# Four layers of cross-attention on one core: tokens laid out by slots of 128, the last group's tokens sent slot by slot, merged values kept in weight buffers

## The chip, the core and the metric

The kernel runs on one core of a Trainium2 chip, everything in fp32 but one small step. A core has a matrix engine (PE, with its weight loads shown apart as PEld), a vector engine (DVE), a scalar engine (ACT), a general one (POOL), and SyncE (SP), which here only issues transfers. Each engine runs its own instructions strictly in order; semaphores hold an instruction until what it needs is there. 16 DMA engines move data between the device memory and the on-chip memory. The latter has 128 partitions, and nearly every tile here spans all of them. The metric is the device time of one execution in microseconds (us). "Before" was measured in three runs; the profile is of one more execution.

## What is computed

2048 tokens of 256 numbers pass through four layers. Each adds a cross-attention over 77 context rows to the tokens, and then a feed-forward. The four differ; the change lies mostly in the last. Cut to it, the reference is:

```python
# layer 3, attention (x: 2 x 1024 x 256, ctx: 2 x 77 x 256, 16 heads)
Q = rope(layernorm(x) @ Wq)                  # 16 heads of 64
K = rope(ctx @ Wk); V = ctx @ Wv             # 4 heads, each used by 4 query heads
scores = Q K^T / 8 + rel_pos_bias[:, abs(i - k)]
scores = where(mask, scores, -1e9)
x = x + concat_heads(softmax(scores) @ V) @ Wo
# layer 3, feed-forward: each token to one of 8 experts, at most 320 tokens each
xf = layernorm(x)
eid = argmax(softmax(xf @ router_w + router_b))
rank = number of earlier tokens with the same eid
valid = rank < 320
y_tok = expert[eid](xf)                      # relu(xf w1 + b1) w2 + b2
yov = relu(xf @ ow1 + ob1) @ ow2 + ob2       # for the tokens that don't fit
out = x + where(valid, y_tok, yov)
```

## The kernel before

**Tokens.** They are cut into 4 groups (`g`) of 512, and a group into 4 slots (`j`) of 128: `xs[g][:, j, :]` is a slot, one token on each partition. Before the change partition `p` and slot `j` hold token 512 g + 4 p + j, so a partition holds four consecutive tokens.

**Order.** The instructions are written as functions per group, slot or head, and a scheduler then reorders them on each engine by a model of their times, within the data's and the buffers' constraints. So the order on an engine is fixed when the kernel is built, but is not that of the source. Transfers of SP stand in one order too: one that waits for a buffer holds all that come after it.

**Weight rooms.** A pool of 6 buffers of 8 KB a partition holds the big weights in turn (`weight(...)`): those of layer 2's feed-forward (gate2T, up2T, down2T), of layer 3's attention (`wkv3`, `wo3`, `wq3`), and then, a megabyte each, the overflow's `ow1`, `ow2` and two for each expert. A load goes out when the tile that had the room has been read for the last time.

**Layer 3's preparation** (`layer3_setup`) runs piece by piece among the pieces of layer 2's feed-forward. It makes the keys (`kblk`), the mask bias (`mb3`) and, for each of the two batches, the product V Wo by head, 1232 rows of 256, which goes to the device memory (`vd`).

**Layer 3's attention** (`layer3_attention`) then begins with loads on SP: the cosines and sines of the queries (`cs`), and `vd` back as `vw` (L913, L916), two tiles of 10 KB a partition in its own pool. After that it is a pipeline over 16 slots (`pipelined`, L1045). In one step, seven stages work on seven successive slots: `ahead` (normalizes and transposes the next group); `queries` (loads the bias tile `rb`, 128 x 16 x 77, L936; adds the mask to it on POOL, L940; query product `pq` on PE, L946; rope on DVE and POOL); `queries_turned` (transposes, L965); `scores` (product, L981; scaling and bias on DVE, L988; softmax by halves of 8 heads, L995 to L1003, whose last step is a multiply on POOL); `last` (`values`: transposes of the weights, L1016, and product with `vw`, L1023, sum into `xs`, L1026); `slot_then` (router logits, for the last group slot by slot, L1117 to L1134, else by group); `after(send)`.

**Sending** (`send`, L1143). For a group: which expert is largest (`largest`), the rank of each token in its expert, whether it overflows, the row that it goes to, and four scatters (L1191), one for each slot, of 513 numbers a token (x, its norm, its index) into the buffer `buf` in the device memory. A rank within the group has two parts: a matmul with a triangular matrix counts the tokens on lower partitions (and one with ones adds `carry`, the count of the groups before); `before` adds up on POOL what the same partition holds in lower slots. The overflow goes the same way with `over` and `os`.

**Experts.** `experts()` reads rows back from `buf` (L1220), for the overflow first (`xe_o`), transposes them (L1229), and runs hidden and answer products for the overflow and the 8 experts. The first read waits for all scatters.

Of the kernel before, what the change touches and what calls it, by code (L numbers as in the profile page):

```python
# [22 lines left out]
F32 = mybir.dt.float32  # L23
# [3 lines left out]
U32 = mybir.dt.uint32  # L27
# [6 lines left out]
P = 128  # L34
D = 256
# [31 lines left out]
def tile_layers(ctx: ExitStack, tc: tile.TileContext, a: dict, out: bass.AP):  # L67
# [26 lines left out]
    def pside(name):  # L94
        return psr.tile([P, 512], F32, tag="pr", name=name)
# [125 lines left out]
    def largest(v, n, name):  # L221

        hot = st.tile([P, J, n], F32, tag="hot", name=f"hot_{name}")
        mx = st.tile([P, J], F32, tag="lmx", name=f"lmx_{name}")
        left = cst[:, C_LEFT : C_LEFT + n].unsqueeze(1).to_broadcast([P, J, n])
        nc.vector.tensor_reduce(mx, v, AX.X, ALU.max)
        nc.vector.tensor_tensor(hot, v, bc(mx, n), ALU.is_equal)
        nc.vector.tensor_tensor(hot, hot, left, ALU.mult)
        nc.vector.tensor_reduce(mx, hot, AX.X, ALU.max)
        nc.vector.tensor_tensor(hot, hot, bc(mx, n), ALU.is_equal)  # L230
        return hot
# [16 lines left out]
    def pipelined(n, *stages):  # L248

        for step in range(n + len(stages) - 1):  # L250
            for k, stage in enumerate(stages):
                if 0 <= step - k < n:
                    stage(step - k)
# [557 lines left out]
    def layer3_setup():  # L811
# [67 lines left out]
        for b, vT in enumerate(vTs):  # L879
# [17 lines left out]
            vds.append(vd)  # L897
        yield wq, mb3, kblk, vds

    def layer3_attention(route, wq, mb3, kblk, vds):  # L900
        with tc.tile_pool(name="a3", bufs=2) as ap, tc.tile_pool(name="a3c", bufs=1) as c3:
            cs = c3.tile([P, 2, 2, J, HD3], F32, name="cs")
            for i in range(2):
# [4 lines left out]
                )  # L908
            vws = []
            for b, vd in enumerate(vds):  # L910
                vw = c3.tile([P, NC3, D], F32, name=f"vw3{b}")
                full = (NC3 - 1) * P
                nc.sync.dma_start(  # L913
                    vw[:, : NC3 - 1, :], vd[:full, :].rearrange("(m p) n -> p m n", p=P)
                )
                nc.sync.dma_start(vw[: H * L - full, NC3 - 1, :], vd[full:, :])  # L916
                vws.append(vw)
            rel = a["relbias"]
# [13 lines left out]
            def queries(it):  # L932
                g, j = divmod(it, J)
                n, gb = f"a3{g}{j}", g % 2
                rb = ap.tile([P, H, L], F32, tag="rb", name=f"rb_{n}")
                nc.sync.dma_start(  # L936
                    rb,
                    bass.AP(rel.tensor, rel.offset + gb * GT + j, [[J, P], [RELW, H], [1, L]]),
                )
# [66 lines left out]
            def values(it):  # L1006
# [15 lines left out]
                for m, w in chunks:  # L1022
                    nc.tensor.matmul(  # L1023
                        po, t[:w, m, :], vws[g // 2][:w, m, :], start=(m == 0), stop=(m == NC3 - 1)
                    )
                nc.vector.tensor_tensor(xs[g][:, j, :], xs[g][:, j, :], po, ALU.add)  # L1026

            def after(f):

                return lambda it: f(it // J) if it % J == J - 1 else None  # L1030

# [12 lines left out]

            pipelined(G * J, ahead, queries, queries_turned, scores, last, slot_then, after(send))  # L1045

# [24 lines left out]
    def layer3_ffn():  # L1071
# [63 lines left out]

        def before(dst, src):

            nc.gpsimd.memset(dst[:, 0], 0.0)
            nc.gpsimd.tensor_copy(dst[:, 1], src[:, 0])
            for j in range(2, J):  # L1140
                nc.gpsimd.tensor_tensor(dst[:, j], dst[:, j - 1], src[:, j - 1], ALU.add)

        def send(g):  # L1143
            n, lg = f"f3{g}", made.pop(g)
            hot = largest(lg, E, n)


            tot = st.tile([P, E], F32, tag="tot3", name=f"tot_{n}")
            nc.vector.tensor_reduce(tot, hot.rearrange("p j e -> p e j"), AX.X, ALU.add)
            pr = pside(f"pr_{n}")[:, :E]  # L1150
            nc.tensor.matmul(pr, tri, tot, start=True, stop=False)
            nc.tensor.matmul(pr, ones, carry, start=False, stop=True)
            nc.vector.tensor_tensor(carry, carry, tot, ALU.add)
            rank = st.tile([P, J, E], F32, tag="rank3", name=f"rank3_{n}")
            before(rank, hot)
            first = st.tile([P, J], F32, tag="first3", name=f"first_{n}")
            sel = st.tile([P, J, E], F32, tag="sel3", name=f"sel_{n}")
            nc.vector.tensor_tensor(
                sel, hot, e320.unsqueeze(1).to_broadcast([P, J, E]), ALU.mult
            )  # L1160
            nc.vector.tensor_reduce(first, sel, AX.X, ALU.add)
            nc.vector.tensor_tensor(
                rank, rank, pr.unsqueeze(1).to_broadcast([P, J, E]), ALU.add
            )
            nc.vector.tensor_tensor(rank, rank, hot, ALU.mult)
            r = st.tile([P, J], F32, tag="r3", name=f"r_{n}")
            nc.vector.tensor_reduce(r, rank, AX.X, ALU.add)

            o = st.tile([P, J, 1], F32, tag="o3", name=f"o_{n}")
            nc.vector.tensor_scalar(o[:, :, 0], r, float(CAP), None, ALU.is_ge)  # L1170
            ot = st.tile([P, 1], F32, tag="ot3", name=f"ot_{n}")
            nc.vector.tensor_reduce(ot, o[:, :, 0], AX.X, ALU.add)
            po = pside(f"pov_{n}")[:, :1]
            nc.tensor.matmul(po, tri, ot, start=True, stop=False)
            nc.tensor.matmul(po, ones, over, start=False, stop=True)
            nc.vector.tensor_tensor(over, over, ot, ALU.add)
            os = st.tile([P, J, 1], F32, tag="os3", name=f"os_{n}")
            before(os, o)

            nc.vector.tensor_tensor(r, r, first, ALU.add)  # L1180
            nc.vector.tensor_tensor(os[:, :, 0], os[:, :, 0], r, ALU.subtract)
            nc.vector.scalar_tensor_tensor(
                os[:, :, 0], os[:, :, 0], po, o[:, :, 0], ALU.add, ALU.mult
            )
            nc.vector.scalar_tensor_tensor(
                r, o[:, :, 0], float(NSLOT), r, ALU.mult, ALU.add
            )
            to = st.tile([P, J], U32, tag="to3", name=f"to_{n}")
            nc.vector.tensor_tensor(to, os[:, :, 0], r, ALU.add)
            for j in range(J):  # L1190
                nc.gpsimd.indirect_dma_start(  # L1191
                    out=next(views),
                    out_offset=bass.IndirectOffsetOnAxis(ap=to[:, j : j + 1], axis=0),
                    in_=tokens[g][:, j, :], in_offset=None,
                )
# [180 lines left out]
    with tc.tile_pool(name="masks", bufs=1) as mp:  # L1376
# [13 lines left out]
        with (  # L1390
# [23 lines left out]
            layer1_attention(weights, beside)  # L1414
            with tc.tile_pool(name="a3s", bufs=2) as sp, tc.tile_pool(name="f2", bufs=2) as fp:
                route, hidden, down = layer2_ffn(fp, gate_up)
                setup.send(sp)


                route(0)  # L1420
                for g in range(G):
                    pieces = [lambda e=e: hidden(g, e) for e in range(E)]
                    pieces += [lambda j=j: down(g, j) for j in range(J)]
                    for k, piece in enumerate(pieces):
                        if g + 2 < G and k < len(chain):
                            chain[k](g + 2)
                        piece()
                        if g < 2 and k % 2 == 1 and k > 4 or (g, k) in ((0, 1), (0, 3)):
                            next(setup)
                        if g + 1 < G and k == E:  # L1430
                            route(g + 1)
                made3 = next(setup)
    route, experts = layer3_ffn()
    layer3_attention(route, *made3)
    experts()

def _constants(np):
# [9 lines left out]
    c[:, C_E320 : C_E320 + E] = CAP * np.arange(E)  # L1449
    token = GT * np.arange(G)[None, :, None] + J * p[:, None, None] + np.arange(J)[None, None, :]  # L1450
    c[:, C_TOKEN : C_TOKEN + G * J] = token.reshape(P, G * J)
# [11 lines left out]


def _laid_out(np, given):
    i = {k: np.asarray(v) for k, v in given.items()}
    o = {k: v for k, v in i.items() if k[0] == "L"}
    o["x"] = i["x"].reshape(NT, D)
    ctx = i["ctx_1024"][:, ::-1]
    o["ctxn"] = ctx  # L1470
    o["ctxT"] = ctx.transpose(2, 0, 1)
    o["mask0"] = i["mask_Bx1xSxS2_bk1"][..., ::-1].reshape(NT, L)
    o["mask1"] = i["mask_Bx1xSxS2_ik1"][..., ::-1].reshape(NT, L)
    o["mask2"] = i["mask_BxSxS2_ik1"][..., ::-1].reshape(NT, L)
    o["mask3"] = i["mask_BxS2_bf1"][:, ::-1]
# [10 lines left out]
    rope = _rope(np)  # L1486
    o["ropeq"] = rope
    o["ropek"] = rope[:, L - 1 :: -1]
# [20 lines left out]
```

## Time and profile before

| | |
|---|---|
| three runs | 1139.82, 1141.12, 1142.36 us (median 1141.12) |
| the profiled execution | 1144.02 us, its span 1141.9 us |
| mean clock granted to PE | 0.957 of full speed |
| PE busy | 1030.9 us, 90% of the span |
| DVE, POOL, ACT busy | 719.7, 384.3, 362.3 us |
| device memory | 55.35 MB read, 19.64 MB written, 66 GB/s |
| from 640 to 701 us (layer 2's feed-forward, end) | PE busy 59.42 of 61.00 us |
| from 701 to 735 us (start of layer 3's attention) | PE busy 28.48 of 34.00 us |
| from 735 to 905 us (most of it) | PE busy 161.12 of 170.00, DVE 133.81, POOL 111.33 |
| from 925 to 946 us (hand-over to the experts) | PE busy 4.88 of 21.00 us, clock 0.62 |
| from 946 us to the end (experts) | PE busy 182.52 of 196.00 us |

The span is that of the instructions; the execution's own time includes what lies around them. In a row of the timeline the first number is the start in us from the beginning of the span, the second its length, then engine, line of the source, operation, output <- inputs, shapes, and "xN" where N alike in a row are put together. The brackets give the idle time of the engine before it and what ended it. "issue" means that the engine waited for nothing that the profile shows. In the row of clocks, and of busy shares, a digit is tenths, and 9 is 90% or more.

### The profile page before, as it was taken

How to read it: one execution, taken by the hardware profiler on the slowest of the kernel's cores; microseconds unless marked ns; L12 is line 12 of the kernel's file. 1: busy time of each engine (PE TensorE's matmuls, PEld its weight loads, DVE VectorE, ACT ScalarE, POOL GpSimd, SP SyncE). 2: the span in 40 equal slices, each digit the busy share in tenths (PEclk: the TensorE clock that was granted, in tenths of full speed). 3: DMA queues.
4: the chain of work that ended last, by engine and by line, in shares of the span. 5: the costliest groups of instructions: out<-in, count | busy, mean ns of one | idle time of the engine just before them, and what ended most of it. 6: DMA issues, size and time to landing. Idle time of an engine off the chain costs nothing.

```text
span 1141.9 us, 13923 instructions
## 1 busy us (share of the span) xinstructions
PE 1030.9 (90%) x4776; PEld 645.4 (57%) x4776; DVE 719.7 (63%) x1849; ACT 362.3 (32%) x1116; POOL 384.3 (34%) x367
## 2 busy tenths in 40 slices
PE   5899989999998887796998999799899958999996
PEld 3355544455444454465664646577678845767774
DVE  6678965776668799949596537668878731222211
ACT  1666620000376563131321110555354511111100
POOL 5633310013333453413120001766566641211211
PEclk9899989999998998897999999999999977999998
DMA  8400038432200000011001005522132223253530
GB/s 266 64 1 1 2 82 143 79 52 45 77 1 1 1 1 28 12 60 48 12 23 60 0 3 184 131 46 56 34 93 62 80 88 93 78 176 100 191 131 18
DMA packets 100279, 74.89 MB, mean 66 GB/s; under 512 B 57916, under 2 KB 90476, under 8 KB 100206
## 3 DMA queue, kind: packets, MB, share of 16 engines
q1 hardware_dynamic: 92974, 58.20, 18.3%
q10 hardware_dynamic: 4800, 9.46, 4.7%
q0 software_dynamic: 2432, 6.31, 1.5%
q8 instruction: 40, 0.66, 0.2%
q14 instruction: 33, 0.27, 0.1%
HBM read 55.35 MB, written 19.64 MB: 66 GB/s over the span
## 4 chain that ended last, share of the span: by engine, by line
PE 59%; DVE 22%; DMA 7%; issue 4%; ACT 4%; POOL 3%; SPq 0%; POOLq 0%; DVEq 0%; ACTq 0%
PE pe_f L548 10%; PE pgu_f L761 8%; PE poe_e L1289 4%; PE po_a L1023 4%; DMA out_x<-ye_e,ids_e 3%; PE pc_a L452 3%; PE ph_e L1269 3%; PE pq_a L946 3%; DVE x L781 3%; PE pPT_a L439 3%; DMA xe_e<-buf 2%; PE po_f L774 2%; PE psc_a L403 2%; DVE x L158 2%; PE pq_a L376 2%
## 5 line engine op out<-in xcount | busy, mean ns | idle before, releaser
L414 ACT ACTIVATE s_a<-psc_a,mx_a 128x77 f32<-128x77 f32 x512 | 121.7, 337 | 65.0 <-DVE mx_a L412 59.4
L421 POOL TENSOR_TENSOR s_a<-s_a,sm_a 128x616 f32<-128x616 f32 x64 | 78.1, 1221 | 122.2 <-DVE sm_a L420 90.0
L548 PE MATMUL pe_f<-ew,xnT_f 128*128 128x512 f32 x256 | 117.0, 605 | 0.0
L554 DVE SCALAR_TENSOR_TENSOR x<-pe_f,gate_f,x 128x256 f32<-128x256 f32 x128 | 61.6, 482 | 41.7 <-PE pe_f L548 39.3
L997 ACT ACTIVATE s_a<-s_a,mx_a 128x77 f32<-128x77 f32 x256 | 67.2, 347 | 62.0 <-DVE mx_a L995 61.8
L548 PEld LDWEIGHTS pe_f<-ew,xnT_f 128*128 128x128 f32 x256 | 47.9, 194 | 54.6 <-issue 52.5
L1023 PE MATMUL po_a<-vw,PT_a 128*128 128x256 f32 (+1 forms) x320 | 77.3, 381 | 0.8 <-ACT PT_a L1018 0.8
L1269 PE MATMUL ph_e<-xT_e,w 128*128 128x320 f32 x256 | 75.6, 436 | 0.0
L774 PE MATMUL po_f<-down2T,hT_f 128*128 128x256 f32 x256 | 65.0, 400 | 8.4 <-DVE x L781 8.3
L412 DVE TENSOR_REDUCE mx_a<-psc_a 128x4 f32<-128x308 f32 x128 | 57.4, 464 | 18.8 <-ACT s_a L414 9.7
L1093 DVE TENSOR_SCALAR hT_e<-ph_e,b1c 128x320 f32<-128x320 f32 (+1 forms) x36 | 20.6, 572 | 75.6 <-PE ph_e L1269 75.6
L946 PE MATMUL pq_a<-wq,xnT_a 128*128 128x512 f32 x128 | 60.3, 609 | 5.7 <-DVE s_a L988 5.7
L761 PE MATMUL pgu_f<-xnT_f,gate2T 128*128 128x512 f32 x128 | 63.5, 619 | 1.0 <-DVE hT_f L767 0.6
L781 DVE SCALAR_TENSOR_TENSOR x<-po_f,cw_f,x 128x256 f32<-128x256 f32 x128 | 60.8, 480 | 5.3 <-PE po_f L774 2.1
L1091 ACT ACTIVATE hT_e<-ph_e,b1c 128x320 f32<-128x320 f32 (+1 forms) x36 | 19.6, 545 | 137.9 <-PE ph_e L1269 137.9
L1023 PEld LDWEIGHTS po_a<-vw,PT_a 128*128 128x128 f32 (+1 forms) x320 | 57.8, 190 | 9.5 <-issue 1.4
L452 PE MATMUL pc_a<-PT_a,vblk_a 128*32 128x256 f32 (+1 forms) x512 | 59.0, 405 | 4.0 <-DVE y_f L643 1.4
L439 PE MATMUL pPT_a<-cst,s_a 128*128 128x128 f32 (+1 forms) x320 | 56.0, 290 | 6.3 <-DVE PT_a L447 4.0
L1289 PE MATMUL poe_e<-w,hT_e 128*128 128x256 f32 x256 | 61.3, 381 | 0.0
L774 PEld LDWEIGHTS po_f<-down2T,hT_f 128*128 128x128 f32 x256 | 48.3, 197 | 22.3 <-DVE x L781 15.0
L761 PE MATMUL pgu_f<-xnT_f,up2T 128*128 128x512 f32 x128 | 60.1, 592 | 0.0
L439 PEld LDWEIGHTS pPT_a<-cst,s_a 128*128 128x128 f32 (+1 forms) x320 | 35.7, 142 | 40.0 <-issue 21.2
(316 smaller groups left out, 1981.1 us busy)
## 6 DMA issues: line engine op xcount, KB each, us to landing
w<-in_L_ffn_w SPq DMA_DIRECT2D x16, 1024.0 KB
rb_a<-in_relbias SPq DMA_DIRECT2D x16, 616.0 KB
buf<-none ACTq DMA_DIRECT2D x12, 769.5 KB
vd<-vo SPq DMA_DIRECT2D x8, 308.0 KB
vw<-vd SPq DMA_DIRECT2D x2, 1152.0 KB
xe_e<-buf SPq DMA_DIRECT2D x8, 257.0 KB
x<-in_x SPq DMA_DIRECT2D x4, 512.0 KB
ew<-in_L_ffn_expert_w SPq DMA_DIRECT2D x4, 512.0 KB
```

The source lines that it names most:

```text
L414: nc.scalar.activation(s[:, c, 4 * i + h, :], sv[:, h, :], AF.Exp, bias=mx[:, h : h + 1], scale=-1.0,)
L421: nc.gpsimd.tensor_tensor(s[:, c], s[:, c], bc(sm, L), ALU.mult)
L439: nc.tensor.transpose(pt[: wide(m), m - m0, k * P : (k + 1) * P], sp[k][:, c, m * P : m * P + wide(m)], ident,)
L452: nc.tensor.matmul(pc[cols, c, :], vblk[g // 2][: wide(m), c, m, cols], t[: wide(m), m, :], start=(k == 0), stop=(k == 1),)
L548: nc.tensor.matmul(pe[:, i, :], xnT[:, kc, j * P : (j + 1) * P], ew[half][:, kc, i * 512 : (i + 1) * 512], start=(kc == 0), stop=(kc == KC ...
L761: nc.tensor.matmul(pgu[:, i, :], wgu[i][:, kc, e * INTER : (e + 1) * INTER], xnTs[g][:, kc, :], start=(kc == 0), stop=(kc == KC - 1),)
L774: nc.tensor.matmul(po[:, e // 2, (e % 2) * D : (e % 2) * D + D], hTs[g, half][:, e, j * P : (j + 1) * P], wd[:, 4 * half + e, :], start=Tr ...
L781: nc.vector.scalar_tensor_tensor(x, po[:, e // 2, (e % 2) * D : (e % 2) * D + D], cws[g][:, j, ee : ee + 1], x, ALU.mult, ALU.add,)
L946: nc.tensor.matmul(pq[:, i, :], xnTs[g][:, kc, j * P : (j + 1) * P], wq[:, kc, i * 512 : (i + 1) * 512], start=(kc == 0), stop=(kc == KC - 1),
L1023: nc.tensor.matmul(po, t[:w, m, :], vws[g // 2][:w, m, :], start=(m == 0), stop=(m == NC3 - 1))
L1269: nc.tensor.matmul(ph[:, h % 2, :rows], w1[:, kc, h * P : (h + 1) * P], xT[:, kc, :], start=(kc == 0), stop=(kc == KC - 1),)
L1289: nc.tensor.matmul(po, hT[:, h, i * P : (i + 1) * P], w2[:, h, :], start=(h == 0), stop=(h == NH - 1),)
```

## The change

1. **Layout.** Partition `p` and slot `j` now hold token 512 g + 128 j + p. The inputs and the masks are permuted on the way in, the sines too, and the table of token indices. The bias of a slot is read with a step of one element from partition to partition instead of four; rows and bytes are the same.
2. **Values.** `vw` no longer has tiles of its own: its 20 pieces of 128 rows lie in three weight rooms, filled during layer 2's feed-forward.
3. **Bias tiles.** The pool `c3`, with `cs` and the two `rb` buffers, is opened before layer 2's feed-forward rather than after it, so that the buffers lie apart from that stage's.
4. **Send.** It takes any run of slots. Since slots now follow each other in token order, the triangular matmul runs on the one-hot of every slot at once, and `so_far` makes the running counts on POOL, which the matmul with ones adds. Group 3 is sent slot by slot (`sent`). The number of scatters stays 16.

```diff
-        yield wq, mb3, kblk, vds
+        rooms = [weight([P, 8, D], f"vw3{i}") for i in range(-(-NB * NC3 // 8))]
+        vws = [[rooms[c // 8][:, c % 8] for c in range(b * NC3, (b + 1) * NC3)] for b in range(NB)]
+        for b, vd in enumerate(vds):
...
+                nc.sync.dma_start(
+                    rooms[c // 8][:, c % 8 : c % 8 + n],
+                    vd[m * P : (m + n) * P, :].rearrange("(m p) n -> p m n", p=P),
+                )
...
+        yield wq, mb3, kblk, vws
...
-                rb = ap.tile([P, H, L], F32, tag="rb", name=f"rb_{n}")
+                rb = c3.tile([P, H, L], F32, tag="rb", name=f"rb_{n}", bufs=2)
                 nc.sync.dma_start(
                     rb,
-                    bass.AP(rel.tensor, rel.offset + gb * GT + j, [[J, P], [RELW, H], [1, L]]),
+                    bass.AP(rel.tensor, rel.offset + gb * GT + j * P, [[1, P], [RELW, H], [1, L]]),
                 )
...
-                        po, t[:w, m, :], vws[g // 2][:w, m, :], start=(m == 0), stop=(m == NC3 - 1)
+                        po, t[:w, m, :], vws[g // 2][m][:w], start=(m == 0), stop=(m == NC3 - 1)
...
-            def after(f):
-
-                return lambda it: f(it // J) if it % J == J - 1 else None
+            def sent(it):
+
+                g, j = divmod(it, J)
+                if g == G - 1:
+                    send(g, j, 1)
+                elif j == J - 1:
+                    send(g)
...
+        def so_far(n, src, total, name, kind):
+
+            cum = st.tile([P, J, src.shape[2]], F32, tag=f"{kind}3", name=name)[:, :n]
+            nc.gpsimd.tensor_copy(cum[:, 0], total)
+            for i in range(1, n):
+                nc.gpsimd.tensor_tensor(cum[:, i], cum[:, i - 1], src[:, i - 1], ALU.add)
+            nc.gpsimd.tensor_tensor(total, cum[:, n - 1], src[:, n - 1], ALU.add)
+            return cum
+
+        def send(g, j0=0, m=J):
+
+            n, lg = f"f3{g}{j0}", made[g][:, j0 : j0 + m]
             hot = largest(lg, E, n)
-            tot = st.tile([P, E], F32, tag="tot3", name=f"tot_{n}")
-            nc.vector.tensor_reduce(tot, hot.rearrange("p j e -> p e j"), AX.X, ALU.add)
-            pr = pside(f"pr_{n}")[:, :E]
-            nc.tensor.matmul(pr, tri, tot, start=True, stop=False)
-            nc.tensor.matmul(pr, ones, carry, start=False, stop=True)
-            nc.vector.tensor_tensor(carry, carry, tot, ALU.add)
...
-            before(rank, hot)
+            pr = pside(f"pr_{n}")[:, : m * E]
+            nc.tensor.matmul(pr, tri, hot.rearrange("p j e -> p (j e)"), start=True, stop=False)
+            cum = so_far(m, hot, carry, f"cum_{n}", "rank")
+            nc.tensor.matmul(pr, ones, cum.rearrange("p j e -> p (j e)"), start=False, stop=True)
...
+            po = pside(f"pov_{n}")[:, :m]
+            nc.tensor.matmul(po, tri, o[:, :, 0], start=True, stop=False)
+            os = so_far(m, o, over, f"os_{n}", "os")
+            nc.tensor.matmul(po, ones, os[:, :, 0], start=False, stop=True)
 
             nc.vector.tensor_tensor(r, r, first, ALU.add)
-            nc.vector.tensor_tensor(os[:, :, 0], os[:, :, 0], r, ALU.subtract)
+            place = st.tile([P, J], F32, tag="ot3", name=f"place_{n}")[:, :m]
             nc.vector.scalar_tensor_tensor(
-                os[:, :, 0], os[:, :, 0], po, o[:, :, 0], ALU.add, ALU.mult
+                place, po, float(NSLOT), r, ALU.add, ALU.subtract
             )
...
+            nc.vector.tensor_tensor(place, place, o[:, :, 0], ALU.mult)
+            to = st.tile([P, J], U32, tag="to3", name=f"to_{n}")[:, :m]
+            nc.vector.tensor_tensor(to, place, r, ALU.add)
+            for i in range(m):
                 nc.gpsimd.indirect_dma_start(
                     out=next(views),
-                    out_offset=bass.IndirectOffsetOnAxis(ap=to[:, j : j + 1], axis=0),
-                    in_=tokens[g][:, j, :], in_offset=None,
+                    out_offset=bass.IndirectOffsetOnAxis(ap=to[:, i : i + 1], axis=0),
+                    in_=tokens[g][:, j0 + i, :], in_offset=None,
                 )
...
-            with tc.tile_pool(name="a3s", bufs=2) as sp, tc.tile_pool(name="f2", bufs=2) as fp:
...
+            with tc.tile_pool(name="a3c", bufs=1) as c3:
+                with tc.tile_pool(name="a3s", bufs=2) as sp, tc.tile_pool(name="f2", bufs=2) as fp:
```

## The prediction

> **What bounds the kernel now.** I read the page first: PE is busy 90% of the span, DVE 63%, POOL 34%. A change that moves no matmul can therefore pay only where PE stands still. The row of forty slices (28.5 us each) shows where that is:
>
> ```profile
> PE   5899989999998887796998999799899958999996
> PEclk9899989999998998897999999999999977999998
> ```
>
> After the start there are two dips that the change touches: slices 24 and 25 (entry to layer 3's attention) and slice 33 (the hand-over from attention to the experts, PE at 5, clock 7). Next I read the waits of PE between 640 and 740 us; columns are who waited, for whom, the sum, how often, the longest:
>
> ```profile
> PE pq_a L946 <- DVE s_a L988: 5.0, 1, 5.0
> ```
>
> One wait of 5 us. The timeline (start, length, engine, line; in brackets the idle time before and what ended it) tells its cause:
>
> ```profile
> 709.58 6.26 SPq L936 DMA_DIRECT2D rb_a<-in_relbias  x2
> ...
> 718.49 2.57 POOL L940 TENSOR_TENSOR rb_a<-rb_a,mb 128x1232 f32<-128x1232 f32 x1 [4.28 <-DMA rb_a<-in_relbias]
> ...
> 721.10 1.51 DVE L988 SCALAR_TENSOR_TENSOR s_a<-psc_a,rb_a 128x616 f32<-128x616 f32 x2 [5.47 <-POOL rb_a L940]
> ...
> 721.95 5.27 PE L946 MATMUL pq_a<-wq,xnT_a 128*128 128x512 f32 x8 [4.96 <-DVE s_a L988]
> ...
> 730.95 3.60 PE L946 MATMUL pq_a<-wq,xnT_a 128*128 128x512 f32 x8
> ```
>
> The bias tile `rb` is issued only at 709.58, behind cs and both vw on SP. Its mask add ends at 721.06, DVE's first score step follows, and frees PE's PSUM. PE then runs cold: eight matmuls take 5.27 us against 3.60 later.
>
> The timeline of the hand-over:
>
> ```profile
> 917.61 1.22 POOL L1003 TENSOR_TENSOR s_a<-s_a,sm_a 128x616 f32<-128x616 f32 x1 [0.89 <-DVE to_f L1189]
> ...
> 919.00 1.13 POOL L1191 DMA_INDIRECT buf<-x,to_f  x1 [0.17 <-DVE stats_f L1118]
> ...
> 926.40 0.21 POOL L1119 TENSOR_SCALAR stats_f<-stats_f 128x1 f32<-128x1 f32 x1 [1.54 <-DVE stats_f L1118]
> ...
> 929.38 0.17 DVE L1134 TENSOR_TENSOR lg_f<-pxs_f,r_L_ffn_router_b 128x8 f32<-128x8 f32 x1 [1.67 <-PE pxs_f L1130]
> ...
> 934.62 0.16 DVE L1189 TENSOR_TENSOR to_f<-os_f,r_f 128x4 uint32<-128x4 f32 x1
> ...
> 939.02 0.96 POOL L1191 DMA_INDIRECT buf<-x,to_f  x1 [0.30 <-issue]
> 943.45 2.23 SPq L1220 DMA_DIRECT2D xe_o<-buf  x5
> ...
> 945.81 1.95 PE L1229 MATMUL px_o<-cst,xe_o 128*128 128x128 f32 x8 [10.58 <-issue]
> ```
>
> So the tail is: last softmax multiply, last slot's statistics, its logits, the send of four slots, four scatters at 1.27 us pitch, 4.43 us from the last one's start to the load, PE. Every us on this chain is a us of the time.
>
> **Part 1: early bias tiles.** cs and the first two rb go to SP near 454 us, before layer 2's feed-forward. The 4.96 us wait goes, and with it the cold run, 5.27 - 3.60 = 1.67: **-6.6 us**. Late next is rb of slot 2: its buffer frees when slot 0's scores are read, near 718; its load may take as long as slot 0's wait shows (issue 709.58, landed 718.4, with the vw traffic ahead), but its scores are wanted only after 730. Ends: -7.5 (SP's and DVE's lesser waits go too) and -3 (half of it comes back as a wait on the next rb).
>
> The adds themselves do not vanish. 2 x 2.57 us of POOL move to about 462 and 467 us, among layer 2's steps, into this place:
>
> ```profile
> 464.55 2.40 POOL L701 TENSOR_TENSOR o_a<-o_a,r_L_xattn_gamma 128x1024 f32<-128x1024 f32 x1 [2.08 <-DVE o_a L158]
> ```
> ```profile
> 464.56 0.16 DVE L212 TENSOR_TENSOR gt_f20g<-gs_f 128x16 f32<-128x16 f32 x1
> 464.65 2.33 DVE L213 TENSOR_TENSOR eq_f20g<-gs_f 128x16 f32<-128x16 f32 x1
> ...
> 469.24 0.67 DVE L767 TENSOR_TENSOR hT_f<-sg_f,pgu_f 128x512 f32<-128x512 f32 x1
> ```
> ```profile
> 469.97 1.99 PE L838 MATMUL pk<-wkv,ctxT 128*77 128x256 f32 x4 [5.22 <-DVE hT_f L767]
> ```
>
> A DVE operation of 0.16 us takes 2.33 beside POOL's multiply, another (467.07) 2.16 beside POOL's add, and hT behind them holds PE for 5.22 us. The Trainium skill, SBUF — State Buffer, section Who interferes with whom, says why, and speaks against this change: a DVE instruction with two SBUF inputs and a GpSimd one that reads SBUF exclude each other for the whole instruction. By that rule each moved add can cost 2.57 on this path, together **+5.1**. By the rows: eight such DVE operations start at 464.39, two or three slip through between two POOL instructions. With the adds on either side of the multiply the POOL run is 462.5-465.05, -467.45, -470.0; hT starts at about 470.2 instead of 469.24: **+1.0**. I take the rows' value. The lower end is -0.5, since the batch-norm steps of group 1 leave this stretch of DVE.
>
> **Part 2: values in weight rooms.** The same 2.3 MB are read during layer 2's feed-forward, where DMA stands at 0 to 2 tenths and PE waits for no load: 0. SP's order then holds them behind rooms that come free, and the overflow's weights move to about 685 and 702 us, 240 us before their use: 0. The first expert's w1 now waits for group 1's last values (about 827), before rb of slot 11 in SP's order; that rb waits for scores read near 838: 0. What is not free is the second expert's 2 MB: before, they were loaded at 715.88 and 881.28; now they wait for the last slot's values and go out among the scatters. Four scatters at 880.85-884.80, beside one such megabyte, landed 6.6 to 10.5 us after issue; the four at the end of the kernel before 3.5 to 4.3. I return to this below.
>
> **Part 3: bias stride.** 2048 rows of 308 bytes in both, only their first addresses lie closer. No row shows the new stride; the nearest is the old load, hidden from slot 2 on. 0, ends ±0.5.
>
> **Part 4: send.** Groups 0 to 2: 14 DVE operations instead of 20, at 0.22 us pitch 1.3 us each, in stretches where DVE is busy 134 of 170 us and PE 161. The wait for `tot` (0.9 us, once) goes, while the second matmul of each pair now waits for POOL's running sum. **-0.5**, ends -3 and +2 (PE's waits there sum to about 8 us).
>
> The last group: the same 16 scatters, but three more DVE chains of 14, with their matmuls and POOL sums, among the last two slots' softmax. The instruction order of the changed kernel shows what they push:
> - On PE, the second half of slot 3's scores stands behind nine po_a matmuls at 0.43: about 3.5 us later than before (912.5 to 916.0, in the old time).
> - On DVE, slot 2's normalisation, which waits for POOL, stands ahead of that half's sum: together the last softmax multiply ends 5.1 us later, 924.0 instead of 918.8.
> - On POOL, group 2's four scatters (5.1 us) follow, then two sums, slot 0's scatter (1.27), four small steps, and only then slot 3's statistics; slot 1's scatter (1.27) stands between these and their power. DVE meanwhile waits in order for slot 1's place. Statistics 932.8 (before 926.4), power ends 934.9, logits 937.2 (before 929.4).
> - The send of one slot: 14 operations, 4.8 us instead of 5.2 (20 operations, 929.57 to 934.78): 942.0. Here the change pays: one scatter, at 942.3, where before the four went from 935.07 to 939.02, so 7.8 us of delay at the logits have become 3.3 at the last scatter. 942.3 + 4.43 = 946.7 against 943.45: +3.3; with the small steps at their shortest +2.4. Say **+3.0**.
> - In DVE's order the `to` of slot 2, which waits until group 2's scatters have landed, stands ahead of slot 3's logits. The last of these is issued near 928, beside the 2 MB: at 5.1 (the median in the old place) nothing is felt, at 10.5 it is 938.4, 1.4 us after the logits are due. **+0.7**, half of it.
>
> PE is idle and at clock 0.5 there in either kernel. Ends of the tail: -4 and +9.5.
>
> **Sum:** -6.6 + 1.0 - 0.5 + 3.0 + 0.7 = **-2.4 us**. The profiled execution took 1144.02 (span 1141.9), so 1141.6 of its kind. The median of the three runs is 2.9 lower than that execution: 1141.12 - 2.4 = **1138.7**. A measurement of this kernel tells 0.2% (2.3 us) from no change, so the line falls on the edge of "faster".
>
> **Rivals.**
> - *The slot-by-slot send pays in full.* For it: the four last scatters are 3 x 1.27 = 3.8 us of bare chain, and the earlier slots' work lies where DVE is half idle. Against: POOL's order above. Tail -3.8 instead of +3.7: -9.9, **1131.2**.
> - *The wait at the entry changes hands.* rb of slot 2, or POOL's q add (2.35, twice, at 708.11 and 711.85), holds PE next. For it: rb of slot 2 was waited for too (1.34 at 727.25). Against: PE stood 4.96 us for one tile alone. Gain 3 instead of 6.6: +1.2, **1142.3**, no change.
> - *The 2 MB behind the last values slow the scatters* (the other side). Place: SP, from 928 on. Group 2's and slot 0's scatters land at 10.5, slot 2's `to` and behind it slot 3's logits wait; and if the last scatter too lands beside them, 10.5 replaces 4.43: tail +3.0 + 6.1 = +9.1. Sum -6.6 + 1.0 - 0.5 + 9.1 = +3.0, **1144.1**. It decides slower from a tail of 8.4 on. For it: the 6.6 to 10.5 us above. Against: 2 MB at the 270 GB/s seen near 885 take 7.8 us, gone by 938.
> - *The adds near 465 cost the rule's 5.1*: +1.7, 1142.8, no change.
>
> **Chances.** My forecast 0.45 (own range 1135 to 1141), full pay 0.12, changed hands 0.10, the rule's price 0.08, slow scatters 0.25. Range: 1131.5 to 1146, which takes in the full pay and the slow scatters with the bounds of the middle; under 2 in 10 lie outside. Faster by over 2.3 us: half of the first and the second and a little more, 0.40. Slower by over 2.3: the slow scatters and the upper ends of the two at 1142, 0.35. Between: 0.25.
>
> **What would show it.** Entry: PE's wait for DVE L988 gone, POOL's rb add no longer waiting for its DMA, eight pq in 3.6. Layer 2: PE's wait for hT before pk, 5.2 now, 6.2 if I am right, over 10 by the rule. Tail: the last L1003 multiply to slot 3's statistics, and from those to the load of xe_o; the load at 3 to 4 us later after the start of layer 3's scores than before. The two w loads behind the last values, and the landing of the scatters beside them. I am wrong if the load of xe_o does not come later, if PE waits at the start of layer 3 for another producer, or if layers 0 to 2 shift by more than 2 us.

## The result, and the profile after

The changed kernel took 1156.98 us (median of 6 runs, 1155.28 to 1164.49) beside 1141.44 us for the kernel before on the same chip: ratio 1.0147, 95% interval 1.0124 to 1.0170. It is slower, by 15.5 us between the medians and some 17 by the ratio, and outside the predicted range. Its profiled execution has a span of 1159.5 us (before 1141.9) at a mean granted clock of 0.949 (0.957).

The row of PE in forty slices, now 29.0 us each:

```profile
PE   5899989999897898495989999999999877999996
```

The dip at the entry to layer 3's attention (slices 25 and 26, counted from 1; the prediction calls them 24 and 25) is gone, as predicted. But slice 17 (464 to 493 us), in layer 2's feed-forward, is at 4 where the kernel before had 7, and the hand-over has spread over slices 32 to 34.

To see where time is lost I matched the same PE instruction in the two traces and took the difference of their starts (after minus before, each from its own span's start):

| PE instruction (start in the kernel before) | after - before, us |
|---|---|
| `pk`, layer 3's keys among layer 2's feed-forward (470.0) | +2.4 |
| `po_f` (544.1) | +7.4 |
| an `up2T` matmul of the next run (556.5) | +15.6 |
| `gate2T` (578.2) | +17.5 |
| last part of layer 2's feed-forward (690.1) | +20.2 |
| `psc_a` in layer 3's attention (772.2) | +12.9 |
| `po_a` (898.5) | +7.7 |
| first `px_o` of the experts (945.8) | +19.0 |
| end of the span (1141.9) | +17.6 |

So the entry and the attention gave back 12.5 us, more than hoped, and two places lost far more: layer 2's feed-forward 20.2, the hand-over 11.3. Up to 453 us, where both kernels run the same instructions in the same order, the differences already lie between -2.2 and +0.7, so a us in a row of this table says nothing.

**Layer 2's feed-forward.** The timeline of the changed kernel (start, length, engine, line), to be held against the rows at 464.55 shown for the kernel before:

```profile
462.72 2.61 POOL L947 TENSOR_TENSOR rb_a<-rb_a,mb 128x1232 f32<-128x1232 f32 x1 [0.54 <-DMA rb_a<-in_relbias]
462.81 3.63 DVE L158 TENSOR_SCALAR o_a<-o_a,mv_a21o,rstd_a21o 128x256 f32<-128x256 f32 x4
...
466.53 2.39 POOL L702 TENSOR_TENSOR o_a<-o_a,r_L_xattn_gamma 128x1024 f32<-128x1024 f32 x1 [1.20 <-DVE o_a L158]
...
466.62 2.33 DVE L213 TENSOR_TENSOR eq_f20g<-gs_f 128x16 f32<-128x16 f32 x1
...
468.88 2.61 POOL L947 TENSOR_TENSOR rb_a<-rb_a,mb 128x1232 f32<-128x1232 f32 x1
468.96 2.57 DVE L213 TENSOR_TENSOR eq_f20g<-gs_f 128x16 f32<-128x16 f32 x1
...
471.62 0.68 DVE L768 TENSOR_TENSOR hT_f<-sg_f,pgu_f 128x512 f32<-128x512 f32 x1
...
472.35 1.99 PE L839 MATMUL pk<-wkv,ctxT 128*77 128x256 f32 x4 [8.52 <-DVE hT_f L768]
...
474.36 2.53 DVE L577 TENSOR_SCALAR lq_f<-x 128x256 bf16<-128x256 f32 x2
...
474.52 2.22 POOL L705 TENSOR_TENSOR x<-x,o_a 128x1024 f32<-128x1024 f32 x1
```

Each long POOL row has a DVE instruction beside it that ends within 0.2 us of it. The first is the surprise: L158 is a normalization with one tile as input. Four of them took 1.37 us at 463.10 before; here they take 3.63, and 2.67 of it is the first alone, which ends at 465.48, POOL's add at 465.32. That delay pushes POOL's multiply from 464.55 to 466.53 and everything behind it. PE waits 8.52 us for hT instead of 5.22.

That is 3.3 us. Behind it the stage is not the old one with a delay: the scheduler has placed it anew. On each engine the trace gives the order of instructions. Matched between the two traces, from 440 to 700 us some 200 of PE's 879 and 230 of DVE's 540 stand in another order, DVE's from 474 us on (four `bns_f<-x`, at 474.6 before, come only at 483.4), PE's from 495. Before 440 us none does.

Then PE loses its clock. Its timeline, and below it the windows view of 550 to 570 us, the changed kernel first (length, busy us and number of instructions of PE, PEld, DVE, ACT, POOL, then granted clock, DMA share, GB/s):

```profile
545.40 2.00 PE L775 MATMUL po_f<-down2T,hT_f 128*128 128x256 f32 x8 [2.91 <-DVE x L782]
...
551.43 3.78 PE L775 MATMUL po_f<-down2T,hT_f 128*128 128x256 f32 x8 [2.09 <-DVE x L782]
...
562.52 3.78 PE L762 MATMUL pgu_f<-xnT_f,gate2T 128*128 128x512 f32 x4
...
569.51 1.88 PE L762 MATMUL pgu_f<-xnT_f,gate2T 128*128 128x512 f32 x4
...
595.72 3.78 PE L762 MATMUL pgu_f<-xnT_f,gate2T 128*128 128x512 f32 x4 [3.47 <-DVE hT_f L768]
```
```profile
550.00:570.00 20.00, 18.57 (x52) 11.86 (x53) 10.08 (x30) 3.79 (x6) 1.26 (x2) 0.57 0.12 39
```
```profile
550.00:570.00 20.00, 20.00 (x74) 11.18 (x73) 7.92 (x19) 8.02 (x14) 1.26 (x2) 1.00 0.05 16
```

Four matmuls of one shape take 3.78 us in the cold stretch and 1.88 after it: PE is busy for 18.6 of 20 us at a clock of 0.57 and gets 52 instructions done instead of 74. Twice, here and at 595.72, a stretch at the low clock follows waits of 2 to 3.5 us. From the stage's start near 453 us to the first `pq` PE is idle for 35.0 us instead of 21.6, and its 826 matmuls keep it busy for 234.6 instead of 226.9 (windows view): of the 21.1 us that this stretch is longer, 13.4 are waits and 7.7 slower matmuls.

**The hand-over.** Two new waits. The bias tile of the last slot went out in the middle of group 1's four scatters (898.82 to 903.73), and PE waited for a softmax multiply that stood on POOL behind the mask add of that tile (timeline around 900 us):

```profile
900.46 0.37 SPq L943 DMA_DIRECT2D rb_a<-in_relbias  x1
...
910.10 2.57 POOL L947 TENSOR_TENSOR rb_a<-rb_a,mb 128x1232 f32<-128x1232 f32 x1 [3.78 <-DMA rb_a<-in_relbias]
...
913.89 1.54 PE L1023 MATMUL pPT_a<-cst,s_a 128*128 128x128 f32 x6 [5.78 <-POOL s_a L1010]
```

and the row numbers `to` of the last group's slot 2 (timeline of the tail):

```profile
941.99 0.37 SPq L1336 DMA_DIRECT2D w<-in_L_ffn_w  x1
942.63 0.96 POOL L1194 DMA_INDIRECT buf<-x,to_f  x1 [0.30 <-issue]
...
947.15 0.48 SPq L1338 DMA_DIRECT2D w<-in_L_ffn_w  x1
...
953.25 0.16 DVE L1192 TENSOR_TENSOR to_f<-place_f,r_f 128x1 uint32<-128x1 f32 x1 [3.74 <-DMA buf<-x,to_f]
...
958.17 0.99 POOL L1194 DMA_INDIRECT buf<-x,to_f  x1 [1.66 <-DVE to_f L1192]
...
962.30 2.23 SPq L1223 DMA_DIRECT2D xe_o<-buf  x5
```

The `to` tile is written into a buffer that an earlier scatter reads; DVE stood 3.74 us until that scatter (the one at 942.63) had landed, with slot 3's logits behind it. Expert 1's two megabytes go out beside it.

### The profile page after: what moved, and what is told of

Read it like the earlier page. It is cut to its first block, busy times and chain, and to the rows that moved or that the text cites. A ratio compares the mean times of both kernels' runs of the same rounds, so it can differ in the third digit from the quotient of the medians.

```text
span 1159.5 us, 14013 instructions
## 1 busy us (share of the span) xinstructions
PE 1042.7 (90%) x4800; PEld 653.8 (56%) x4800; DVE 727.4 (63%) x1867; ACT 362.9 (31%) x1116; POOL 388.2 (33%) x381
## 4 chain that ended last, share of the span: by engine, by line
PE 59%; DVE 22%; DMA 8%; issue 3%; POOL 3%; ACT 3%; ACTq 0%; SPq 0%; POOLq 0%; DVEq 0%
PE pe_f L549 10%; PE pgu_f L762 8%; PE poe_e L1292 4%; PE ph_e L1272 4%; PE pq_a L953 4%; PE po_a L1030 4%; DMA out_x<-ye_e,ids_e 3%; DVE x L782 3%; PE pc_a L453 3%; PE pPT_a L440 3%; DVE x L158 2%; PE psc_a L404 2%; PE po_f L775 2%; DMA xe_e<-buf 2%; PE pq_a L377 2%
## 5 line engine op out<-in xcount | busy, mean ns | idle before, releaser
L1030 PE MATMUL po_a<-vw,PT_a 128*128 128x256 f32 (+1 forms) x320 | 81.2, 394 | 0.8 <-ACT PT_a L1025 0.7
L762 PE MATMUL pgu_f<-xnT_f,gate2T 128*128 128x512 f32 x128 | 66.3, 642 | 7.5 <-DVE hT_f L768 5.5
L762 PE MATMUL pgu_f<-xnT_f,up2T 128*128 128x512 f32 x128 | 62.5, 612 | 0.0
L151 POOL TENSOR_SCALAR rstd_a<-mv_a 128x4 f32<-128x4 f32 x16 | 4.3, 269 | 170.8 <-DVE mv_a L150 170.8
L768 DVE TENSOR_TENSOR hT_f<-sg_f,pgu_f 128x512 f32<-128x512 f32 x32 | 21.9, 684 | 59.7 <-ACT sg_f L767 59.7
```

Source lines behind the costliest of these rows:

```text
L762: nc.tensor.matmul(pgu[:, i, :], wgu[i][:, kc, e * INTER : (e + 1) * INTER], xnTs[g][:, kc, :], start=(kc == 0), stop=(kc == KC - 1),)
L1030: nc.tensor.matmul(po, t[:w, m, :], vws[g // 2][m][:w], start=(m == 0), stop=(m == NC3 - 1))
```

## The experiments

Ratios are to the kernel before on the same chip, with 95% intervals. It took 1143.5 us beside held, scat, held_scat and held_scat_to, 1142.3 beside hs_to6, hs_w, hs_whole and best, 1144.1 beside dve, best_whole and best2.

### held: the two mask adds out of the middle of layer 2

```diff
-                nc.gpsimd.tensor_tensor(
-                    rb, rb, mb3[:, g // 2, :].unsqueeze(1).to_broadcast([P, H, L]), ALU.add
-                )
+                with tc.issue_after(gated["pow"]) if it < 2 else ExitStack():
+                    nc.gpsimd.tensor_tensor(
+                        rb, rb, mb3[:, g // 2, :].unsqueeze(1).to_broadcast([P, H, L]), ALU.add
+                    )
```

They are queued on POOL behind the power of the last norm before layer 3 (about 615 us), so the tiles are still early.

> The changed kernel, with the mask adds of the first two bias tiles queued on POOL behind the last normalization power that layer 2 leaves there (near 613 us), where POOL then stands idle; the loads stay early. Theory A (the two moved adds hold the port that DVE needs in layer 2's feed-forward, and PE then runs cold): PE's wait for hT before pk falls from 8.5 to about 5.2 us, the matmul pq of slot 2 comes 17 to 21 us earlier, time 1136 to 1141 us. Rival B (the loss between 470 and 620 us comes from the order that the value rooms bring, on SP and in the schedule): no more than 3 us gained, time 1154 to 1158.

Measured: 1.0062 (1.0042 to 1.0082), span 1149.9. The first `pq` starts at 706.5 instead of 721.9 (before 701.7): 15.5 of the 20.2 us are gone. At 463.75 four L158 take 1.38 us again. The adds in that place are the cause, and not an order that the value rooms bring (rival B): from 440 to 700 us PE, DVE, ACT and POOL run their instructions in exactly the order of the kernel before, the two adds apart. The same holds for every run below but scat and dve. So held takes away two things at once, the adds beside DVE's rows and the new order that came with them. The time is above theory A's 1136 to 1141, for the hand-over costs 15.0 us here instead of 11.3. What is left in layer 2 is the same effect where the adds stand now. PE is 0.6 us late up to 614.8 and 4.7 from 640 on; in held_scat, below, which has the same edit, the two adds run from 614.55 to 619.7, and

```profile
614.55 5.16 POOL L949 TENSOR_TENSOR rb_a<-rb_a,mb 128x1232 f32<-128x1232 f32 x2
614.60 5.90 DVE L158 TENSOR_SCALAR x<-x,mv_a,rstd_a 128x256 f32<-128x256 f32 x4 [1.46 <-POOL rstd_a L152]
...
620.42 1.27 DVE L768 TENSOR_TENSOR hT_f<-sg_f,pgu_f 128x512 f32<-128x512 f32 x2
621.15 2.92 PE L762 MATMUL pgu_f<-xnT_f,gate2T 128*128 128x512 f32 x4 [2.10 <-DVE hT_f L768]
```

four L158 last 5.90 us, PE waits 2.10 for hT and runs cold (2.92 for a run of 1.88).

### dve: the same adds at the same place, on VectorE

```diff
-                nc.gpsimd.tensor_tensor(
+                (nc.vector if it < 2 else nc.gpsimd).tensor_tensor(
```

> The changed kernel with one edit: the mask adds of slots 0 and 1, which stand in layer 2's feed-forward there, run on VectorE instead of GpSimd, at the place that the order gives them. Theory A1, what layer 2 loses comes from a long GpSimd add running at the same time as VectorE's instructions (each is held until the other is done): without it the feed-forward's rows keep their length of the kernel before (x4 of the normalizing tensor_scalar near 463 about 1.4 us instead of 3.6), layer 2 loses only VectorE's own 1.5 to 2.7 us per add, and the first pq comes near 705 to 711 instead of 721.9; time 1144 to 1151. Rival A2, the loss is that the adds take queue time at a place where everything waits, whatever engine they are on: first pq near 716 or later, time 1153 or more.

Measured: 1.0076 (1.0050 to 1.0102), 1152.49 us; first `pq` at 711.0. The timeline of DVE in this run:

```profile
463.06 1.37 DVE L158 TENSOR_SCALAR o_a<-o_a,mv_a21o,rstd_a21o 128x256 f32<-128x256 f32 x4
...
470.61 1.43 DVE L947 TENSOR_TENSOR rb_a<-rb_a,mb 128x1232 f32<-128x1232 f32 x1
...
473.30 1.50 DVE L947 TENSOR_TENSOR rb_a<-rb_a,mb 128x1232 f32<-128x1232 f32 x1
```

The first `pq` is at the upper end of A1's stretch and the time between the two theories. Without POOL's adds beside DVE 9.3 of the 20.2 us stay, of which 2.9 are the adds' own length, so the holds are not the whole cost. But the 10.9 us that go are not the price of the holds either: this run has a third order of PE's and DVE's instructions in the stage, neither that of the kernel before nor that of the changed one. No run has the changed kernel's order without the holds.

### scat and held_scat: group 1's scatters ahead of slot 14's mask add

```diff
+                with tc.issue_after(gated["sent", 1]) if it == 14 else ExitStack():
+                    nc.gpsimd.tensor_tensor(
...
-                nc.gpsimd.indirect_dma_start(
+                gated["sent", g] = nc.gpsimd.indirect_dma_start(
```

This is POOL's order of the kernel before. scat is the changed kernel with that edit alone, held_scat has that of held too.

> The changed kernel, with group 1's four scatters queued on POOL ahead of slot 14's mask add, as before the change; nothing else. Theory C (slot 15's bias load is slow because it meets these scatters, and POOL then holds the softmax multiplies that PE waits for): the load lands in 5 instead of 9.6 us, PE's wait of 5.8 us near 914 goes, time 1149 to 1152 us. Rival D (the load is late because a megabyte of weights stands just ahead of it on SP): the wait stays at 4 us or more, time 1155 to 1159.

> Both edits together. If A and C both hold and do not hide each other: about 1131 to 1135 us, that is 6 to 10 us below the kernel before. If A holds and D: as the held adds alone. If B holds: 1148 or more.

scat: 1.0143 (1.0121 to 1.0166), no gain, outside both theories. PE's wait of 5.8 us is gone, but one of 6.3 us for the norm of group 2, which stands behind slot 15's mask add, has taken its place. The last `po_a` came 5.3 us earlier (939.1 instead of 944.4), but the first `px_o` at 965.4, not earlier than 964.8: slot 2's `to` now waits 6.81 us instead of 3.74. Slot 15's tile itself is still slow: issued at 900.45, its add begins at 908.99, 8.5 us later, while the kernel before took 5.2 (890.66 to 895.89), its load going out 5.9 us after the last of group 1's scatters. In scat the megabyte of weights went out 10 us ahead of it, so the scatters beside it are the likelier cause; that was not tried alone. held_scat: 1.0013 (1.0001 to 1.0025), 4.9 parts in a thousand better than held, so on top of held the edit is worth 5 to 6 us (why it is worth nothing alone stays open); the 1131 to 1135 us hoped for are missed by over 10. Its tail now shows:

```profile
938.88 0.16 DVE L1194 TENSOR_TENSOR to_f<-place_f,r_f 128x1 uint32<-128x1 f32 x1 [6.39 <-DMA buf<-x,to_f]
```

### held_scat_to and hs_to6: more buffers for `to`

held_scat with 4, and with 6, buffers instead of 3 (`tag="to3", bufs=4`).

> As both edits together, and four buffers instead of three for the row numbers `to`, so that slot 2's row numbers no longer wait for the landing of group 2's scatters. Theory E (DVE's 3.7 us wait there holds the last slot's logits): 3 to 4 us less than both edits together. Rival F (the last slot's statistics, held on POOL behind scatters, set the end anyway): less than 1 us gained.

> held_scat with six buffers for to (row numbers of the scatters) in place of three, so that no slot of the last group waits for the landing of an earlier scatter before its row numbers are written. Theory E2, that write's wait itself sets the end: px of the overflow rows begins 4 to 6 us earlier and the time is 1140 to 1142. Rival F2, the landing of the scatters sets it, the wait only shows it early: the load of the overflow rows waits for the same landing, px moves by less than 2 us, and the time is 1144 to 1146 (four buffers gave 1145.7).

With 4: 1.0019 (1.0010 to 1.0028), nothing; slot 3's `to` waits 4.02 us in place of slot 2's. With 6: 1.0005 (0.9992 to 1.0017), so at most 1 us, not told apart from held_scat. No `to` waits any more, and the wait has gone to the load:

```profile
946.54 2.21 PE L1234 MATMUL px_o<-cst,xe_o 128*128 128x128 f32 x8 [10.11 <-DMA xe_o<-buf]
```

The buffers only decide where the late landing is felt.

### hs_w: expert 1's weights behind the overflow rows

```diff
+                    with tc.issue_after(gated["rows"]) if e == 1 else ExitStack():
+                        w1 = weight([P, KC, HID], f"w1_{e}")
...
```

held_scat with the two 1 MB loads queued behind the loads of `xe_o` (`gated["rows"]`).

> The two mended orders of held_scat (mask adds of slots 0 and 1 held to the end of layer 2's norms, group 1's scatters ahead of slot 14's add), and expert 1's two weight loads (1 MB each) queued on SyncE behind the first load of the overflow rows instead of ahead of it. Against held_scat 1145.9 beside 1143.5 of the kernel before. Theory G, the 2 MB share the engines with the scatters and double their landing: the scatters issued from 921 on land in about 4 to 5 us instead of 11 to 15, slot 2's to waits under 1 us instead of 6.4, px of the overflow rows begins about 6 us earlier (near 942 instead of 948.5), and the time is 1139 to 1141, unless expert 1 then waits for its weights, which a wait of its first matmul would show. Rival H, the scatters are slow by themselves[...]: slot 2's to still waits 4 us or more, px stays within 1.5 us of 948.5, and the time is 1145 to 1147.

Measured: 0.9979 (0.9970 to 0.9988), 3.4 parts in a thousand better than held_scat, and 0.2% faster than the kernel before. In held_scat the eight scatters from 920.96 on took 11.9 us in the median from issue to landing (DMA view, 915 to 945 us); in the kernel before, in that stretch, 4.3; in hs_w 4.0:

```profile
buf<-x,to_f POOLq DMA_INDIRECT x8, 11.9
```
```profile
buf<-x,to_f POOLq DMA_INDIRECT x8, 4.3
```
```profile
buf<-x,to_f POOLq DMA_INDIRECT x8, 4.0
```

With the weights out of the way, the tail of hs_w:

```profile
926.61 0.96 POOL L1196 DMA_INDIRECT buf<-x,to_f  x1 [0.31 <-issue]
...
935.48 0.16 DVE L1194 TENSOR_TENSOR to_f<-place_f,r_f 128x1 uint32<-128x1 f32 x1 [1.29 <-DMA buf<-x,to_f]
...
938.09 0.99 POOL L1196 DMA_INDIRECT buf<-x,to_f  x1 [0.94 <-DVE to_f L1194]
...
942.04 2.23 SPq L1225 DMA_DIRECT2D xe_o<-buf  x5
```

Slot 2's `to` is free 8.9 us after group 2's last scatter was issued, not 14.0 as in held_scat (924.92 to 938.88). From group 2's `to` to the first `px_o` it takes 22.1 us instead of 28.0. Theory G is right, rival H wrong; the wait is 1.3 us, not under 1 as written, and `px_o` comes 4.1 us earlier than in held_scat (944.3), not 6. Nor do the experts miss their weights: from `px_o` to the end it is 195.9 us, before 196.1.

### hs_whole and best_whole: the last group sent whole

held_scat, and best (next), with one send of four slots behind the last slot.

> held_scat with the last group sent in one go of four slots behind its last slot, as the other groups are, instead of slot by slot. Theory I, sending slot by slot shortens what lies between the last slot's logits and the last scatter: without it px of the overflow rows begins 2 to 6 us later than held_scat's 948.5 and the time is 1148 to 1152. Rival K, the slot-by-slot sends put waits for landings into VectorE's row and are worth nothing: px within 2 us of 948.5 or earlier, and the time is 1142 to 1146.

> best (1137.1) with the last group sent in one go of four slots behind its last slot. With expert 1's weights out of the way, is the slot-by-slot send worth something? Theory I2, it is, and only the weights hid it: from group 2's to to the first px of the overflow rows it takes 21.9 us in best and 28.4 in the kernel before; whole it takes 25 to 27 here, and the time is 1140 to 1143. Rival K2, it is worth nothing here too: 21 to 23 us and 1136 to 1138.

hs_whole: 1.0015 (1.0007 to 1.0024), no different from held_scat, as K had it. best_whole: 0.9973 (0.9965 to 0.9981) against 0.9956 for best, and 25.7 us from group 2's `to` to `px_o` against 21.9. So the slot-by-slot send is worth nothing beside the weights, and where they are out of the way 3.8 us in the trace and about 2 in the times, whose intervals overlap a little.

### best and best2: a version that beats both

best has all of it: group 1's scatters first, six `to` buffers, late weights, and the mask adds of slots 0 and 1 behind the rope add of their own slot, out of layer 2 altogether.

```diff
+                after = {0: "rope", 1: "rope", 14: ("sent", 1)}.get(it)
```

> All of it mended: the mask adds of slots 0 and 1 queued on GpSimd behind the same slot's rope add, so none lies in layer 2's feed-forward (in held_scat two still do, near 615 to 620), group 1's scatters ahead of slot 14's add, six buffers for to, and expert 1's weights behind the overflow rows' load. If the cold stretch near 621 is what layer 2 still loses in held_scat (about 4 us against before at the first attention row), the first pq comes near 702 to 703 and s_a of slot 0 waits 1 to 3 us more for its add (4.96 us in the kernel before): net gain 1 to 3 us at the last po. With theory G right the tail gives 5 us more: 1134 to 1138, below the kernel before. With rival H right: 1142 to 1145, no better than before.

> best with slot 15's mask add queued on GpSimd behind the pow of group 2's norm instead of ahead of it (there the pow waits 3.5 us for slot 15's bias tile and the add, and TensorE 6.4 us for that norm). Theory L: the wait at 893 shrinks by 3 to 5 us, but the last slot's scores stay bound to its own add, so that 1 to 4 us arrive at the last scatter: 1133 to 1136. Rival M: the last slot's chain (bias tile, add, scores) sets the end and not the norm: 1136 to 1138.

best: 1137.13 us, 0.9956 (0.9939 to 0.9972). Its entry, where the kernel before had eight cold `pq` in 5.27 us after a wait of 4.96:

```profile
700.23 10.57 PE L960 MATMUL pq_a<-wq,xnT_a 128*128 128x512 f32 x24
...
708.92 2.58 POOL L942 TENSOR_TENSOR rb_a<-rb_a,mb 128x1232 f32<-128x1232 f32 x1
...
715.87 3.60 PE L960 MATMUL pq_a<-wq,xnT_a 128*128 128x512 f32 x8
```

No wait, no cold run, and layer 2 untouched (first `pq` 700.2, before 701.7). The early tile needs only its load early, not its add. best2 also takes the norm of group 2 from behind slot 15's add: PE's wait of 6.4 us there vanished, and the time did not move (0.9951, 0.9932 to 0.9970). That is what rival M expected, that the last slot's own chain sets the end.

## Why the prediction was wrong, step by step

| step of the sum | predicted | between the two traces |
|---|---|---|
| adds among layer 2's steps | +1.0 | +20.2 |
| entry to the attention | -6.6 | -7.3 (20.2 to 12.9) |
| middle, three group sends | -0.5 | -5.2 (12.9 to 7.7) |
| tail, its chain and the `to` wait | +3.0 + 0.7 | +11.3 (7.7 to 19.0) |
| experts | 0 | -1.4 |
| sum | -2.4 | +17.6 |

**The adds: the step that failed.** "With the adds on either side of the multiply ... hT starts at about 470.2 instead of 469.24: +1.0. I take the rows' value." hT started at 471.62, and PE's wait before `pk` grew by 3.3 us, not 1.0. Two errors made 20 us of that.

First, I counted only the DVE rows with two inputs as held, and so had POOL's multiply begin at 465.05, where it began at 466.53. The section Who interferes with whom of SBUF — State Buffer in the Trainium skill, which I had quoted for two inputs, says further on that a `tensor_scalar` can take the shared pair too; the rows agree, 3.63 us for four instead of 1.37, and 5.90 in held_scat. Even the 5.1 us of that rule was a quarter of the cost.

Second, and this is the larger part, I stopped the count at hT and let the rest of the stage stand as it was. The prediction reads the changed kernel's instruction order for the tail and says nothing of it for layer 2, where the scheduler had moved nearly a quarter of PE's matmuls. PE's waits grew by 13.4 us in all, the first included, and slower matmuls made 7.7 more: behind waits of 2.91 and 2.09 us the delay grew from 7.4 to 15.6 us (544.1 to 556.5 of the old time) without a further wait, most of it at a clock near half. held and best show that the adds in this stage are the cause: moved to its end 15.5 us are gone, taken out all of it. How the waits divide between holds and new order isn't told apart by these runs.

Of the signs that I had named, PE's wait for hT came out at 8.5 us, between my 6.2 and the rule's 10; and layers 0 to 2 shifted by 20 us, where I had called over 2 a sign of being wrong.

**The entry: right**, wait and cold run gone. In the changed kernel the fourth slot's eight `pq`, which had waited 4.96 us and then taken 5.27, follow without a wait:

```profile
737.04 3.60 PE L953 MATMUL pq_a<-wq,xnT_a 128*128 128x512 f32 x8
```

**The middle: right in sign, ten times too small.** In the kernel before, the send of group 0 stood beside the mask add of a bias tile and the rope add behind it, one element a partition in 2.22 us (timeline of POOL, then of DVE):

```profile
817.74 2.58 POOL L940 TENSOR_TENSOR rb_a<-rb_a,mb 128x1232 f32<-128x1232 f32 x1 [3.67 <-DMA rb_a<-in_relbias]
...
820.28 2.34 POOL L807 TENSOR_TENSOR q_a<-q_a,r_a 128x1024 f32<-128x1024 f32 x1
```

```profile
818.12 2.22 DVE L1176 TENSOR_TENSOR over<-over,ot_f 128x1 f32<-128x1 f32 x1
...
820.26 2.38 DVE L1182 SCALAR_TENSOR_TENSOR os_f<-os_f,pov_f,o_f 128x4 f32<-128x4 f32 x1
```

Between 806.78 and 831.81 of the old time the changed kernel gains 3.6 us (+12.9 to +9.3), and so do all the other runs, which share this send. I had costed the removed DVE operations at their undisturbed 0.22 us. No run isolates this; it is read from rows.

**The tail: the chain right but 1.6 us too short, the transfers wrong.** With the weights out of the way (hs_w, best) the tail costs 5.3 and 5.1 us by the measure of the table, where +3.7 was predicted, and its steps are those read from the instruction order: relative to `po_a` at 898.5, the last softmax multiply of hs_w comes 5.4 us later than before (predicted 5.1), slot 3's logits 8.7 (7.8), the load of `xe_o` 5.4 (3.3). The other 6 us of the changed kernel's 11.3 (as much as lies between held_scat, 11.3, and hs_w) are the rival of the two megabytes, priced at 6.1 for another reason. That the figures agree is luck: I had let the last scatter land late, but it landed in 4.1 us (958.17 to 962.30), and the time went to DVE's wait for the older ones. My argument against, that the 2 MB take 7.8 us, did not hold: in held_scat, where they go out at 921.07 and 925.11, the DMA engines are busy for 90% of the time up to 944 us, and eight scatters land in 11.9 us beside them instead of 4.0. Slot 15's bias tile, which I had not looked for at all, cost PE a wait of 5.8 us, but scat shows that mending this alone moved nothing.

**The sum.** The range came from the tail and the entry; the layer-2 term had ends of -0.5 and 5.1. Even the rule's price and the slow scatters together, -6.6 + 5.1 - 0.5 + 9.1 = +7.1, are less than half of the 17.6. What is missing is layer 2's.

Not tried: the early bias tiles without the values in weight rooms; the new stride alone. Where POOL waited for a tile between 765 and 830 us, it took from issue to add 4.4, 4.5 and 5.8 us before and 4.5 to 5.0 after, so the rows show no gain from the stride.

## What to carry to other kernels

An add moved "into idle time" of one engine must be costed against every instruction of the other engine that it can hold, one-input ones too. Where a scheduler orders the instructions, two moved adds can reorder the whole stage: compare its order before and after, and follow the delay until the matrix engine's waits are those of before. In a stage at 90% PE, waits of 13.4 us came with 7.7 us of slower matmuls. Where a load is wanted early, move the load and leave its arithmetic at its use. And a buffer that is held longer starts the next load into it later: look at what lands on the critical path beside that load, and queue the load behind what is needed first.

## What the runs showed that I had not expected

- A DVE normalization (one SBUF tile and two columns in, 128x256 fp32) beside a POOL add: four in 3.63 and 5.90 us, alone 1.37.
- Two adds at another place changed the order of some 200 matmuls and 230 DVE instructions behind them.
- Short waits were followed by a low clock: PE worked some 3.3 us between waits of 2.91 and 2.09 us, and its granted clock was 0.57 from 550 to 570 us, though it was busy for 18.6 of these 20.
- A scatter of 128 rows of 513 numbers landed in 4.3 us in the median at the end of the kernel before, and in held_scat in 11.9 us beside 2 MB of loads; a later one of that run again in 4.2 (941.76, and the load that waits for it at 945.98).
